# Two heads to a quadrant in two attentions of an eight-layer kernel: row maxima and row sums inside the main products, with a way through DRAM

## The chip, the cores and the metric

The kernel runs on one core of a Trainium2 chip. A core has TensorE (matrix products, into PSUM), VectorE, ScalarE, GpSimd and SyncE, each with its own in-order queue, and 16 DMA engines. DMAs are issued from the queues of SyncE, ScalarE and GpSimd. The metric is the device time of one execution in microseconds; the median of the runs is given. All data is float32.

## The reference, cut to what matters

Four pairs of layers (attention, then feed-forward) are applied in turn to 8 x 512 tokens of 128 features. Each sublayer's input is normalised and its output added to the stream. The change is in the first two attentions and in what the second feed-forward needs before it starts.

```python
# layer 0 attention: 16 heads of 8; in every window of 128 queries the mask
# keeps key j <= i with i counted from the window's start, so only the first
# 128 keys count
scores = einsum('bhqd,bhkd->bhqk', wq, wk) * scale
mask = triu(ones((ws, end), dtype=bool), k=1)
attn = softmax(where(mask, neg, scores), axis=-1)
outs.append(einsum('bhqk,bhkd->bhqd', attn, wv))        # then out @ Wo

# layer 1 attention: 16 heads of 8, 64 features to a head
qf = relu(q @ Wf + bf); kf = relu(k @ Wf + bf)
kv = einsum('blhf,blhd->bhfd', kf, v)
out = einsum('blhf,bhfd->blhd', qf, kv)
normalizer = maximum(einsum('blhf,bhf->blh', qf, kf.sum(axis=1)), 1e-06)
out = (out / normalizer) @ Wo + bo

# layer 1 feed-forward: the best of 16 experts for each token, and a shared one
```

## The kernel before

**One loop for layers 0 and 1.** `l0_l1_ffn` runs the first three sublayers and the second feed-forward's router batch by batch (8 batches of 512 tokens, `P` = 128 partitions, `C` = 4 blocks of 128 tokens). A batch goes through generators, each of which yields between steps: `scores` (normalise, q, k, v, row maxima), then calls of `exps` and `add_up` for r = 0 to 3, then `give` (divide, project with Wo, add), `experts` (layer 0 feed-forward), `features` (layer 1 attention) and `router`. One loop counts `t` from `-LEAD`; a batch has N = 8 values of t, "steps" in the text: `exps(b, r)` is called at t = 8b + 2r, the sums follow one and two steps later, `scores(b)` starts `LEAD` steps ahead, and at each t every live generator is moved by one step. Thus at the same time one batch is in its exponentials, a later one in its scores, earlier ones in experts, features and router. After t = 65 steps of the shared expert (`shared`) fill in. The framework gives every engine a fixed order of instructions close to this program order, and sets all waits.

**Quadrants.** A product with 32 rows or 32 columns uses a quarter of TensorE's array, and four such products, on the four quadrants (`quad(q)`), run side by side. A quadrant holds four heads of 8. To pick head r out of it, `kb[:, r]` is k times a mask `m4` that is zero outside the head.

**Layer 0 attention.** In `scores`, line 486 forms the scores with queries on partitions, ScalarE copies them out (492), GpSimd masks them (493), and VectorE takes the negative maximum of each row (497). The maxima are transposed into `mxT`. In `exps`, line 516 forms the scores again with keys on partitions: for each q the product of `kb` and `qT`, and onto it that of `to_all` and `mxT`, which adds the negative maximum. ScalarE takes exp (523), GpSimd masks (525). In `add_up`, line 539 multiplies `eT` with `vq` (v, zero outside the own head) and, one step later, with `own` (ones instead of v); both accumulate over the four r into `o0` and `o1`. In `give`, VectorE takes the reciprocal of the sums (547) and multiplies (549); two steps later come the projection (554) and the addition.

**Layer 1 attention.** In `features`, line 739 forms kf times v and kf times ones (`one`), for all four heads of a quadrant at once (256 columns), line 744 masks the blocks that belong, a transpose gives `kt`, and line 756 multiplies with qf twice: for the normaliser and for the numerator, each a sum over two halves. Lines 761 to 765 divide; two steps later comes the projection (770).

**The zeros.** Rows of tokens are scattered by expert into `rows_in` in DRAM (`f_in`, 71,680 rows of 512 bytes, line 814, GpSimd's indirect DMA). It must be zero before. Lines 830 to 837 do it with ten DMAs of SyncE, one per step, from the zeroed tile `we`, which `experts` later writes (642). After these, one weight of the list `later` is loaded per step (839).

**The rest.** The experts' products, the layers 2 and 3 with their state-space scan (line 1818) and the output follow after this loop and are not touched. Their line 1182 stores `xh` on ScalarE's queue, and line 1246 loads it again on SyncE's.

## Time and profile before

| | |
|---|---|
| median of 3 runs | 1769.04 us (1764.4 to 1776.76) |
| profiled execution, its own time | 1777.53 us |
| its span, first to last instruction | 1775.8 us |
| mean granted TensorE clock | 0.924 of full |
| TensorE busy | 1523.8 us, 86% |
| VectorE busy | 1208.0 us, 68% |
| ScalarE busy | 785.0 us, 44% |
| GpSimd busy | 675.7 us, 38% |
| start of the layer 0 reciprocal, batches 0 to 7 | 64.9, 94.3, 142.0, 191.1, 273.4, 346.7, 416.6, 478.3 us |

A row of a group has the line, the engine, the operation, the tiles (written <- read), the shapes and the count; after the first bar the busy time in us and the mean of one in ns; after the second the idle time of the engine just before, and what ended it. Busy time of products is modelled and counts overlapping ones once. A row of a stretch has its limits and length, and for each engine the busy time and the number of instructions in it.

### The profile page before, as it was taken

The numbers are of one execution on the slowest core, as the hardware profiler recorded it, in microseconds if no ns is written. First come the engines' busy times: TensorE is split into PE (matmuls) and PEld (weight loads), VectorE is DVE, ScalarE is ACT, GpSimd is POOL, SyncE is SP. The second block draws the span as 40 slices with busy tenths as digits, with TensorE's granted clock in tenths as the row PEclk, the third lists the DMA queues.
The fourth block names the chain that finished last, engine by engine and source line by source line (L and its number), as shares of the span: only waits on it lengthen the run. The fifth ranks groups of instructions, "written<-read, shape, count | busy, mean of one in ns | idle before, by whom it ended". The sixth has DMA issues, their size and how long they took to land.

```text
span 1775.8 us, 22525 instructions
## 1 busy us (share of the span) xinstructions
PE 1523.8 (86%) x8133; PEld 672.7 (38%) x8133; DVE 1208.0 (68%) x2305; ACT 785.0 (44%) x1121; POOL 675.7 (38%) x729
## 2 busy tenths in 40 slices
PE   6978898889999887767999899787888988988877
PEld 2322333334444433554455455332222222333335
DVE  5667647655566543235667665559999999998865
ACT  4545545554454342224223123025555645655644
POOL 5644343342322123021212523425456546641670
PEclk8989888988999998988899899899999999999999
DMA  7990000000000002730554374254444444443301
GB/s 265 383 326 24 1 1 1 13 18 7 7 13 20 17 21 68 222 111 20 127 130 115 100 144 111 80 125 124 140 125 130 129 129 126 126 123 96 82 18 30
DMA packets 98944, 170.92 MB, mean 96 GB/s; under 512 B 11592, under 2 KB 41680, under 8 KB 94736
## 3 DMA queue, kind: packets, MB, share of 16 engines
q1 hardware_dynamic: 94112, 158.20, 31.7%
q0 software_dynamic: 3568, 9.18, 1.7%
q10 hardware_dynamic: 1152, 2.10, 0.4%
q8 instruction: 64, 1.05, 0.2%
q14 instruction: 48, 0.39, 0.1%
HBM read 116.50 MB, written 52.95 MB: 95 GB/s over the span
## 4 chain that ended last, share of the span: by engine, by line
PE 45%; DVE 26%; issue 8%; SPq 6%; DMA 5%; POOL 5%; ACT 4%; DVEq 0%; POOLq 0%; ACTq 0%
DVE h L1818 11%; PE key L1572 5%; PE acc L1550 5%; SPq L833 5%; PE bx L1807 3%; PE sT L516 2%; PE gu L366 2%; PE mm L262 2%; PE o L539 2%; PE Z L1618 1%; DMA gx<-du_d 1%; PE mm L739 1%; PE sc L486 1%; DVE zx L1626 1%; PE mm L1178 1%
## 5 line engine op out<-in xcount | busy, mean ns | idle before, releaser
L1818 DVE TENSOR_TENSOR_SCAN h<-a,bx 128x1024 f32<-128x1024 f32 x192 | 426.5, 2268 | 23.9 <-PE bx L1807 23.7
L1813 ACT ACTIVATE a<-dr,nA 128x1022 f32<-128x1022 f32 x192 | 219.3, 1146 | 217.9 <-DVE h L1818 217.7
L1807 PE MATMUL bx<-gx,wb 64*128 64x512 f32 x768 | 218.8, 662 | 62.4 <-DVE h L1818 59.6
L1263 POOL TENSOR_TENSOR gx<-gx,xk 128x1024 f32<-128x1024 f32 x32 | 75.4, 2358 | 222.2 <-DMA gx<-du_d 212.7
L1572 PE MATMUL key<-xT,L_ffn_keys 128*128 128x512 f32 x256 | 139.6, 628 | 20.2 <-DVE act L1576 20.1
L1807 PEld LDWEIGHTS bx<-gx,wb 64*128 64x128 f32 x768 | 64.6, 194 | 195.6 <-DVE h L1818 149.1
L1550 PE MATMUL acc<-act,L_ffn_values 128*128 128x512 f32 x256 | 134.6, 610 | 0.0
L1576 DVE SCALAR_TENSOR_TENSOR act<-key,gate 128x512 f32<-128x512 f32 x128 | 86.5, 684 | 49.3 <-PE key L1572 37.4
L525 POOL TENSOR_SCALAR_AFFINE_SELECT eT<-eT 128x1024 f32<-128x1024 f32 x64 | 68.6, 1094 | 111.2 <-ACT eT L523 111.2
L1618 PE MATMUL Z<-h,wc 64*32 64x512 f32 x1536 | 109.8, 624 | 1.1 <-DVE h L1818 1.1
L497 DVE TENSOR_REDUCE mx<-sm 128x8 f32<-128x1024 f32 x64 | 76.3, 1212 | 48.1 <-POOL sm L493 48.1
L1361 POOL DMA_INDIRECT back<-f_out,back_at x32 | 30.8, 963 | 167.6 <-DVE bn L248 136.2
L493 POOL TENSOR_SCALAR_AFFINE_SELECT sm<-sm 128x1024 f32<-128x1024 f32 x64 | 69.3, 1096 | 57.9 <-ACT sm L492 57.6
L492 ACT COPY sm<-sc 128x1024 f32<-128x1024 f32 x64 | 63.0, 1013 | 58.7 <-PE sc L486 40.3
L523 ACT ACTIVATE eT<-sT 128x1024 f32<-128x1024 f32 x64 | 62.1, 1020 | 56.6 <-PE sT L516 56.5
L486 PE MATMUL sc<-kb,qT 32*128 32x512 f32 x256 | 61.5, 786 | 23.8 <-ACT eT L523 10.2
L1572 PEld LDWEIGHTS key<-xT,L_ffn_keys 128*128 128x128 f32 x256 | 48.0, 198 | 72.6 <-issue 38.2
L1338 ACT COPY oT<-acc 128x512 f32<-128x512 f32 x8 | 4.7, 586 | 159.3 <-PE acc L1550 159.3
L1550 PEld LDWEIGHTS acc<-act,L_ffn_values 128*128 128x128 f32 x256 | 49.9, 197 | 62.0 <-issue 62.0
L516 PE MATMUL sT<-qT,kb 32*128 32x512 f32 x256 | 57.1, 683 | 14.4 <-ACT sm L492 7.6
L248 DVE BATCH_NORM_STATS2 bn<-x 128x6 f32<-128x128 f32 x224 | 56.2, 271 | 6.5 <-DMA x<-in_L_attn_hidden_states 5.4
L1044 POOL TENSOR_TENSOR rstd<-rstd,minus_half 128x4 f32<-128x4 f32 x27 | 28.0, 1039 | 80.7 <-DVE rstd L1043 80.5
(457 smaller groups left out, 3081.2 us busy)
## 6 DMA issues: line engine op xcount, KB each, us to landing
f_in<-we SPq DMA_DIRECT2D x10, 3584.0 KB
gate<-gates SPq DMA_DIRECT2D x128, 256.0 KB
dr<-dt_d SPq DMA_DIRECT2D x32, 1024.0 KB
gx<-du_d SPq DMA_DIRECT2D x128, 128.0 KB
wt<-in_L_ffn_experts SPq DMA_DIRECT2D x48, 192.0 KB
xk<-xh_d SPq DMA_DIRECT2D x32, 256.0 KB
xg<-f_in SPq DMA_DIRECT2D x48, 64.0 KB
f_out<-ys SPq DMA_DIRECT2D x12, 256.0 KB
```

What stands on the lines that cost most here:

```text
L486: nc.tensor.matmul(halves[q // 2][:, 4 * (q % 2) : 4 * (q % 2) + 4, :], qT[quad(q), cols(c)], kb[quad(q)], start=True, stop=True,)
L497: nc.vector.tensor_reduce(mx[:, c, 2 * i : 2 * i + 2, 0:4], sm.rearrange("p (q r) k -> p q r k", q=2), AX.X, ALU.max, negate=True,)
L516: nc.tensor.matmul(halves[q // 2][:, q % 2, :], lhs[quad(q), r, :], rhs[quad(q)], start=(k == 0), stop=(k == 1),)
L833: nc.sync.dma_start(rows_in[per * (t - 1) : per * t, :].rearrange("(p n j) d -> p n (j d)", p=P, j=4), we.rearrange("p c k e -> p (c k e)" ...
L1263: nc.gpsimd.tensor_tensor(gx, gx, xk.unsqueeze(1).to_broadcast([P, 2, S]), ALU.mult)
L1550: nc.tensor.matmul(acc, f2_v[:, j, :], act, start=(j == 0), stop=(j == J - 1))
L1572: nc.tensor.matmul(key, f2_k[:, 2 * j : 2 * j + 2, :], xT, start=True, stop=True)
L1576: nc.vector.scalar_tensor_tensor(act, key, 0.0, gate[:, j % 2, :], ALU.max, ALU.mult)
L1618: nc.tensor.matmul(zs[q][32 * j : 32 * j + 32, i, :], wcf[half, g, :], hs[j // 2][half, j % 2, :], start=(g == 0), stop=(g == G - 1),)
L1807: nc.tensor.matmul(bx[:, k, :], wbf[half, g, :], gx[half, j, :], start=True, stop=True,)
L1813: nc.scalar.activation(a[:, :, 1:], dr[:, 2 * j : 2 * j + 2, 1:], AF.Exp, scale=nA[:, q, g : g + 1],)
L1818: nc.vector.tensor_tensor_scan(h.rearrange("p r t -> p (r t)"), a.rearrange("p r t -> p (r t)"), bx.rearrange("p r t -> p (r t)"), 0.0, AL ...
```

## The change

**Two heads to a quadrant, maxima in the same product.** q is stored to DRAM so that 16 of the 32 rows of a quadrant hold two heads, and two more rows hold these heads' negative maxima; two loads (`qm`) bring both forms back, one for the first and one for the second pair of heads. `k2` has k of one head in its 8 rows and a one in the row of that head's maximum; it is made from a second projection with a padded weight `wk2`. `exps` then needs one product for each q instead of two. `qs`, the two DRAM buffers, are zeroed once at the start.

**Sums in the same product.** `vq` has 32 columns for two heads: 8 of v, 8 of ones, for each. The sums of r = 0, 1 and r = 2, 3 go to two accumulators; each is copied out by ScalarE, stored to DRAM from ScalarE's queue (`halves_out`), and `rejoined` loads numerators and denominators back as two tiles. The reciprocal comes one step after these loads. Layer 1's attention is built in the same way: `v1` has v and ones side by side, a product has 128 columns instead of 256, line 756's products are half as many, and the result goes through DRAM; its division comes two steps after the loads, its projection one step later than before.

**Zeros in groups.** 35 DMAs of 1 MB, seven at each of t = 2, 10, 18, 26, 34, from a tile `nought` of 1 KB per partition, a column of which GpSimd rewrites from the newest `eT` before each group. The weights of `later` follow after the last group. `LEAD` is 14 instead of 13.

The diff, cut to its core:

```diff
+                wk2 = keep.tile([P, 2, 4, 32], F32, tag="wk2", name="wk2")
...
+                qs = [dram.tile([4, 2, 32, S], F32, tag=f"qs{i}", name=f"qs{i}") for i in range(2)]
+                for t in qs:
+                    nc.scalar.dma_start(
+                        t.rearrange("q r x (h t) -> (q r x h) t", h=2).rearrange("(n p) t -> p n t", p=P),
+                        nought.unsqueeze(1).to_broadcast([P, 4, 2 * D]),
+                    )
...
+                def halves_out(od, r, o, ov):
+                    nc.scalar.copy(ov, o)
+                    nc.scalar.dma_start(od[:, r], ov)
+
+                def rejoined(od):
+                    vd = work.tile([P, 2, S], F32, tag="vd", name="vd", bufs=3)
+                    src = od.rearrange("q r (e s d) t -> (q r e) s d t", e=2, s=2)
+                    for s in range(2):
+                        nc.sync.dma_start(vd[:, s], src[:, s])
+                    return vd
...
+                    nc.scalar.dma_start(rows[:, 0:16, :], qT)
...
+                    for i in range(2):
+                        nc.tensor.matmul(
+                            mm[:, cols(2 + i)], wk2[:, i].rearrange("p q x -> p (q x)"), xT[:, 0:P],
+                            start=True, stop=True,
+                        )
...
+                    k2 = work.tile([P, 2, 2, P], F32, tag="k2", name="k2", bufs=2)
+                    for e in range(2):
+                        nc.vector.tensor_scalar(
+                            k2[:, :, e, :], mm[:, 2 * P :].rearrange("p (r k) -> p r k", r=2),
+                            ones_at, mk[:, e : e + 1], ALU.add, ALU.mult,
+                        )
...
+                    nc.scalar.dma_start(rows[:, 16:18, :], mxT)
+                    qm = []
+                    for i in range(2):
+                        qm.append(work.tile([P, S], F32, tag=f"qm{i}", name="qm"))
+                        nc.sync.dma_start(qm[i], qs[b % 2][:, i])
...
-                    for k, (lhs, rhs) in enumerate(((kb, qT), (to_all, mxT))):
-                        for q in range(4):
-                            nc.tensor.matmul(
-                                halves[q // 2][:, q % 2, :], lhs[quad(q), r, :], rhs[quad(q)],
-                                start=(k == 0), stop=(k == 1),
-                            )
+                    for q in range(4):
+                        nc.tensor.matmul(
+                            halves[q // 2][:, q % 2, :], k2[quad(q), r // 2, r % 2, :],
+                            qm[r // 2][quad(q)], start=True, stop=True,
+                        )
...
                         nc.tensor.matmul(
-                            o[quad(q)], vq[:, q, r, :] if i == 0 else own[:, r, :],
-                            eT[q // 2][:, q % 2, :], start=(r == 0), stop=(r == 3),
-                        )
+                            o[quad(q)], vq[:, q, r, :], eT[q // 2][:, q % 2, :],
+                            start=(r % 2 == 0), stop=(r % 2 == 1),
+                        )
+                    if r % 2:
+                        od, ov = sums_of[b]
+                        halves_out(od, i, sums_of.pop((b, i)), ov[:, i])
...
                 def give(b):
                     ready.pop(b)
-                    nc.vector.reciprocal(rd, sums_of.pop((b, 1)))
...
+                    vd = rejoined(sums_of.pop(b)[0])
+                    yield True
+                    aT, rd = vd[:, 0], vd[:, 1]
+                    nc.vector.reciprocal(rd, rd)
+                    nc.vector.tensor_tensor(aT, rd, aT, ALU.mult)
...
-                    for k in (1, 0):
-                        for i in range(2):
-                            for q in range(4):
-                                nc.tensor.matmul(
-                                    o[quad(q), k, :], kt[:, 2 * k + i, quad(q)], qf[:, q, i, :],
-                                    start=(i == 0), stop=(i == 1),
-                                )
+                    for i in range(2):
+                        for q in range(4):
+                            nc.tensor.matmul(
+                                o[quad(q), i, :], kt[:, i, quad(q)], qf[:, q, i, :],
+                                start=True, stop=True,
+                            )
+                    od = dram.tile([4, 2, 32, S], F32, tag="od1", name="od1", bufs=2)
+                    ov = work.tile([P, 2, S], F32, tag="vd", name="ov", bufs=3)
+                    nc.scalar.copy(ov, o)
+                    for i in range(2):
+                        nc.scalar.dma_start(od[:, i], ov[:, i])
+                    vd = rejoined(od)
+                    yield True
+                    yield True
...
-                LEAD = 13
+                LEAD = 14
...
+                    if t % 8 == 2 and t > 0 and fills:
+                        nc.gpsimd.tensor_scalar(
+                            nought[:, 0:1], last[0][:, 0, 0:1], 0.0, None, ALU.mult
+                        )
+                        for rows in (fills.pop() for _ in range(7)):
+                            nc.sync.dma_start(
+                                rows.rearrange("(p n j) d -> p n (j d)", p=P, j=2),
+                                nought.unsqueeze(1).to_broadcast([P, PER // (2 * P), 2 * D]),
+                            )
+                    elif t > 0 and not fills and later:
+                        nc.sync.dma_start(*later.pop(0))
...
-                        if (b, r) in waiting:
-                            add_up(b, r, 1, waiting[b, r])
```

## The prediction

> **What bounds the kernel now.** I read the slices of the page first, then the kernel cut at the ends of the first attention's batches, then the chain of one such batch, then the groups that the change touches, and last the queue that carries the fills. The cuts are the starts of the eight reciprocals of line 547 (64.9, 94.3, 142.0, 191.1, 273.4, 346.7, 416.6, 478.3 us); the loop's last work ends near 665 us. In the stretches the columns are TensorE (PE), its weight loads, VectorE, ScalarE, GpSimd, then the granted clock, the DMA share and GB/s.
>
> ```profile
> 65.00:94.00 29.00, 27.84 (x185) 10.77 (x186) 22.24 (x39) 18.22 (x22) 19.65 (x20) 1.00 1.03 383
> 94.00:142.00 48.00, 36.81 (x198) 12.96 (x196) 29.54 (x66) 21.62 (x26) 21.79 (x23) 0.82 0.89 282
> 142.00:191.00 49.00, 40.76 (x219) 14.27 (x218) 32.89 (x81) 25.67 (x32) 24.21 (x26) 0.90 0.00 0
> 191.00:273.00 82.00, 73.27 (x414) 28.17 (x408) 46.25 (x112) 40.83 (x48) 28.74 (x31) 0.85 0.00 1
> 273.00:347.00 74.00, 65.50 (x406) 27.38 (x406) 46.57 (x110) 38.02 (x47) 27.22 (x30) 0.91 0.02 8
> 417.00:478.00 61.00, 57.15 (x366) 25.28 (x362) 34.59 (x97) 28.26 (x35) 21.11 (x24) 0.89 0.03 10
> 478.00:665.00 187.00, 168.00 (x956) 80.75 (x950) 110.93 (x295) 83.47 (x106) 42.70 (x51) 0.93 0.05 17
> ```
>
> TensorE is busy 77 to 96% of every stretch, VectorE at most 77% (65:94), ScalarE and GpSimd less. So TensorE comes first, but with 4 to 11 us of idle time per batch that other engines' chains make. The chain of waits from 273 to 347 us says the same: products are its largest part (10.9% on line 516, 6.3% on 539, 4.9% on 739), yet from 330 to 347 us it runs through short VectorE steps of the first experts' gating and the two 3.3 us reciprocals, which the change keeps. Work taken from TensorE is therefore worth something in every batch, but not all of it.
>
> ```profile
> L516 PE MATMUL sT<-mxT,to_all 32*128 32x512 f32 x256 | 53.6, 636 | 0.0
> L539 PE MATMUL o<-eT,own 128*32 128x512 f32 x256 | 45.3, 650 | 0.0
> L756 PE MATMUL o<-qf,kt 128*32 128x512 f32 x256 | 29.4, 595 | 3.1 <-ACT sm L492 2.3 <-ACT kt L265 0.8
> L739 PE MATMUL mm<-kf,v 128*32 128x256 f32 x256 | 17.9, 403 | 0.4 <-ACT lg L786 0.4
> L739 PE MATMUL mm<-kf,one 128*32 128x256 f32 x256 | 16.0, 379 | 0.0
> ```
>
> These rows (groups by shape, 0 to 700 us; a product is two records) are the work that goes or halves: busy us, mean ns, idle before.
>
> **The change part by part.** *Score products.* The pass that adds the maxima (to_all by mxT) goes: four products in each of 32 calls. The row says 53.6 us, 1.68 a call, but the four run side by side and the records' ends overlap: at full clock their two waves start 0.43 us apart, so 0.86 us, 0.97 at the stage's clock of 0.89. I take 1.35, between: 32 x 1.35 = 43 us. *Sums.* The products with own go: 45.3 us by the row; a call of lines 539's two sets takes 8.74 us for eight sets in 65:94 (1.09 each) and 10.2 to 10.5 for eight later (1.3). I take 1.25: 40 us. *Linear attention.* The 64 records of line 739 per batch stay, on 128 columns instead of 256: 33.9 us halved is 17, less something for short products: 15. Line 756 goes from 32 to 16 records a batch: 29.4 halved, 15. *Added.* Two products of 128 columns with wk2 per batch: line 466's like product costs 0.46 us a batch, so 8 x 0.93 = 7, less overlap, 5. Two transposes of km fewer a batch (5.1 us halved): -2.5. TensorE's sum is 43 + 40 + 15 + 15 - 5 + 2.5 = **110 us**; bounds 85 (pitch alone) and 132 (all the busy time).
>
> *Beside other work.* VectorE loses vq (0.68) and half of km (0.35) and gains two k2 (256 elements from PSUM, some 0.35 each) and two small copies: zero. ScalarE gains two copies of 512 columns (2 x 0.59) and six DMA issues (0.33 each, the row below) per batch, and half a microsecond for the double-width copy of o: 4 us on 38 of 74, hidden by TensorE. If that cover went, it would be 30 us in all. The set-up adds some ten GpSimd fills of 0.1 to 0.5 us: 3 us beside the wait for the weights.
>
> *The way through DRAM.* Each batch stores qT, mxT and o and loads qm and vd back, and its linear part does so once more. The nearest rows are the scan's store on ScalarE's queue and the load that waits for it:
>
> ```profile
> L1182 ACTq DMA_DIRECT2D xh_d<-xh x8: 326/326/345, 991.2 to 1527.5; - x8
> L1246 SPq DMA_DIRECT2D xk<-xh_d x32: 516/525/631, 993.7 to 1647.8; - x32
> ```
>
> The first store is issued at 991.2 us and SyncE's load at 993.65: 2.4 us. A load lands some 2.8 us after issue (the first x: 0.81 to 3.58). With two issues the round trip is 2.4 + 1.0 + 2.5 = 6 us. For the scores it has two steps of an eighth of a batch (8 to 18 us): hidden. For the sums it has one step before the reciprocal and two before line 554: copy 0.6 + 6 + reciprocal 3.35 + product 0.6 = 10.5 against two steps of 8 to 9 in the early batches (late by 1 to 2 us, three times: 4 us), nothing later. In the linear part it has two steps before the reciprocal: hidden while a step is 7 to 9 us, about 1 us late in each of the four batches of the tail, where it is 3.8 (187 us over 49 steps): 4 us. Its projection also comes one step later, felt once at the end: 4 us. What waits behind on VectorE when vd is late is mx and kf, and TensorE behind those.
>
> *The fills.* Now ten DMAs of 3.5 MB run from 19 to 115 us, and the first write of we waits for them:
>
> ```profile
> L833 SPq DMA_DIRECT2D f_in<-we x10: 1773/9242/10037, 19.4 to 92.3; - x10
> DVE we L642 <- DMA L_ffn_shared_up_w<-in_L_ffn_shared_up_w: 11.8, 1, 11.8
> ```
>
> That wait ends at 120 us (its label is the queue's next transfer). It goes; TensorE is idle 11 us in that stretch against 8 in the next, so I credit 3. After, 35 fills of 1 MB in five groups of seven follow exps of batches 0 to 4, in packets of 1 KB. The trace has 27 ns for 512 bytes, 65 for 1536 and 86 for 2048; in between 46 ns, so a group is 7 x 64 x 46 ns = 20.6 us. Bounds: 19.2 (the rate of 383 GB/s) and 38.5 (a packet costs 86 ns whatever its size). SyncE's queue is in order: qm of the next batch, asked for four steps after the group, stands behind it. With a period T, the load comes at T/4 + 2 (the eT that gates it) + 20.6 + 4, and is needed at T: T is at least 35 us. That binds only in 65:94, now 29 us: +6. (At 38.5 us a group T is at least 59, which would put the first three periods at +30, +11 and +10: the whole change near zero. It goes into the range.) Later loads now start at step 35; the first user (the router of batch 0, near step 44) is behind that. A store on ScalarE's queue during a fill: with busy SyncE traffic xh_d's packets were spread over 8 to 9 us instead of 0.8, but there against packets of 8 KB. The Trainium skill (DMA: Bandwidth & Descriptors, Queues, rings and completion order) says an engine alternates between queues packet by packet; then small fill packets cost a store 1 us. By the row each exposed store would cost 8, by the rule 1. I take the rule, since those 8 KB packets are unlike these; only mxT's store would matter, and its load is behind the fills anyway.
>
> *The clock.* The skill (TensorE: Matmul & The Clock Gate, Part 1) speaks against the change: after an idle window of some 3.4 us TensorE runs at half clock. If each of the 16 round trips left it idle so long, a half-clock window of 3.4 us would cost 1.7 us each: 27 us. The rows show 1.00 where idle is 1 us, 0.82 at 11, but also 0.85 at 9 and 0.90 at 8. Since other products fill these steps, I take nothing beyond the share below.
>
> **The sum.** Per full batch 110/8 = 14 us leave TensorE. What of it is on the chain of 273 to 347: 516's 8.1 us times 1.35/3.46, half of 539's 4.7, half of 739's 3.6, under 1 of 756's: 7 to 8. So between 7.5 and 14; I take 10. Stretches: 0 to 65: -2. 65 to 94: +6. To 142: -7 - 3. To 191: -8. The next three -10 each, to 478: -9. The tail has four linear parts left, 4 x 3.8 = 15 on a TensorE that is 90% busy: -13. Delays from DRAM +4 and +4, last step +4. Together **-54 us**. The profiled execution took 1777.53 us; the median is 1769.04. 54 us off the median: **1715 us**. Nothing after 665 us changes.
>
> **Rivals.** *TensorE really is the bound*: the 132 us of busy time and the wait on we go almost whole, 100 to 125 us: 1655. For it: 94 to 96% busy in 65:94 and 417:478. Against: VectorE's 47 us of 74 with in-order chains. Chance 0.13. *The gain stays off the chain*: only the gating chain counts, 5 us a batch, 40 us, and DRAM (12), fills (6) and clock (27 by the rule) take it back: 1774. For: 330 to 347 us runs without TensorE. Chance 0.13. *The way through DRAM stands in line.* The place is VectorE's queue at the two reciprocals, where vd is awaited; mx and kf stand behind, and TensorE behind them. The price is a whole round trip of 6 us in each of 16, 96 us where I counted 8: 88 us worse, 1803. It decides from where the 54 us are used up: 8 + 54 over 16, that is 3.9 us late each time. For: queues in order, one step of slack before give's reciprocal, and SyncE's queue shared with fills and weights. Against: a step of 6 to 9 us from batch 2 on is as long as the trip. Chance 0.14. *My forecast* (gains of 18 to 100 us): 0.60.
>
> **How the numbers follow.** Faster than 1% (18 us) is about what a measurement can tell from none. Faster: the forecast and the first rival, 0.73; within 1%: 0.13; slower: 0.14. The range takes the bounds of TensorE's sum below and reaches into no gain above: 1650 to 1780.
>
> **What would show it.** After: line 516 and 539 with half their records; the starts of give's reciprocal some 10 us closer from the fourth batch on, and 6 us further apart between the first two; no wait of we; the tail near 185 us; the scan unchanged. Wrong if VectorE waits for vd above 2 us a batch, if TensorE's first score products wait for qm above 3 us in the full batches, or if the stretches shrink by under 5 us.

## The result, and the profile after

The kernel after takes **1894.13 us** (median of 4, 1890.17 to 1898.64) against 1770.38 us for the kernel before on the same chip: a ratio of 1.070 [1.065, 1.074], 124 us slower. The forecast was 1715. The profiled execution took 1898.64 us, with a span of 1896.9 and a mean granted clock of 0.862.

The stretches, cut as before at the starts of the layer 0 reciprocal (now line 614: 100, 161, 212, 268, 350, 427, 505, 568 us). The columns are those of the prediction's first fence.

```profile
0.00:100.00 100.00, 52.47 (x200) 19.45 (x200) 36.30 (x85) 35.78 (x41) 40.36 (x77) 0.77 0.64 188
100.00:161.00 61.00, 46.34 (x152) 15.99 (x148) 30.05 (x67) 25.18 (x31) 25.85 (x29) 0.61 0.49 157
161.00:212.00 51.00, 36.10 (x150) 13.22 (x151) 30.18 (x68) 26.60 (x33) 21.97 (x24) 0.70 0.56 181
212.00:268.00 56.00, 45.38 (x184) 18.55 (x182) 32.83 (x79) 25.27 (x34) 22.28 (x25) 0.74 0.51 167
268.00:350.00 82.00, 64.25 (x302) 27.43 (x302) 44.90 (x98) 37.85 (x45) 25.51 (x27) 0.73 0.36 119
350.00:427.00 77.00, 62.71 (x338) 27.54 (x336) 46.07 (x112) 39.91 (x49) 27.30 (x30) 0.81 0.15 46
427.00:505.00 78.00, 61.95 (x300) 29.09 (x299) 43.34 (x103) 36.43 (x44) 28.70 (x30) 0.68 0.16 45
505.00:568.00 63.00, 50.24 (x288) 23.58 (x285) 34.70 (x99) 30.11 (x36) 18.21 (x22) 0.79 0.14 43
568.00:800.00 232.00, 175.87 (x871) 88.88 (x872) 107.86 (x311) 83.53 (x109) 56.08 (x86) 0.79 0.12 35
```

The count of TensorE's instructions (the first number in brackets) fell as it should: 302 where 414 stood in the fifth stretch. But TensorE is now busy in 71 to 81% of the batches from the second on, where it was 77 to 96%, and the clock column reads 0.61 to 0.81 where it read 0.82 to 1.00. No stretch became shorter. Nearly all the loss lies in the loop of layers 0 and 1: the 32nd scatter of the router, the loop's last work, moved from 688 to 805 us; from there to the end it is 1092 us after and 1088 before.

The groups by shape: first the two rows of the kernel before that the prediction did not show (0 to 700 us), then the kernel after, 0 to 805 us (line 574 was 516, 601 was 539, 805 was 739, 824 was 756):

```profile
L516 PE MATMUL sT<-qT,kb 32*128 32x512 f32 x256 | 57.1, 683 | 14.4 <-ACT sm L492 7.6 <-DVE kf L713 5.6 <-ACT qf L730 0.8
L539 PE MATMUL o<-eT,vq 128*32 128x512 f32 x256 | 44.6, 659 | 0.0
```

```profile
L574 PE MATMUL sT<-qm,k 32*128 32x512 f32 x256 | 79.4, 864 | 58.0 <-DMA qm<-qs 46.8 <-ACT sm L544 6.1 <-ACT qf L794 4.8
L601 PE MATMUL o<-eT,vq 128*32 128x512 f32 x256 | 49.6, 776 | 0.0
L805 PE MATMUL mm<-kf,v 128*32 128x128 f32 x512 | 20.8, 316 | 4.1 <-DVE x L386 3.9 <-ACT v L649 0.2
L824 PE MATMUL o<-qf,kt 128*32 128x512 f32 x128 | 17.6, 656 | 0.2 <-ACT kt L819 0.2
```

The products with the maxima and with `own` are gone. What is left got longer: a record of the score product takes 864 ns, 683 before; one of the sums 776, where it was 650 and 659. And the score product waits 46.8 us for `qm`. The waits of VectorE and of SyncE's queue, 0 to 805 us (total, times, longest):

```profile
DVE vd L837 <- DMA vd<-od: 64.8, 8, 11.9
DVE vd L614 <- DMA vd<-od: 41.1, 4, 16.3
...
SPq L563 <- DMA qs<-mxT: 163.7, 8, 45.8
SPq L494 <- DMA od<-ov: 159.3, 17, 24.0
```

VectorE waits for the rejoined sums in all eight linear parts (64.8 us) and in four of the eight divisions (41.1). With `qm` that is 152.7 us of waits behind the way through DRAM, where the prediction had counted 8. A wait of an engine is not yet time of the kernel. The chain of waits of one batch (268 to 350 us) shows that here it is on the path: the store of `od` and the load of `vd` are 18.7% of it, 15.3 of 82 us.

```profile
by line: issue 16.8%; DMA od<-ov 14.2%; PE sc L538 11.1%; PE sT L574 7.6%; DVE kf L777 5.6%; DMA vd<-od 4.5%; PE mm L735 4.4%; DVE vd L614 4.0%; DVE mx L549 2.9%; ACT qf L794 2.7%; PE o L601 2.5%; PE mm L505 2.4%; PE mm L262 2.3%; ACT kf L7
```

What it is worth in all, experiments had to price.

### The profile page after: what moved, and what is told of

Same layout as the page of the kernel before. It is cut to its first block, busy times and chain, and to the rows that moved or that the text cites. A ratio compares the mean times of both kernels' runs of the same rounds, so it can differ in the third digit from the quotient of the medians.

```text
span 1896.9 us, 21537 instructions
## 1 busy us (share of the span) xinstructions
PE 1522.6 (80%) x7509; PEld 685.5 (36%) x7509; DVE 1211.7 (64%) x2332; ACT 795.8 (42%) x1134; POOL 679.1 (36%) x741
## 4 chain that ended last, share of the span: by engine, by line
PE 45%; DVE 19%; DMA 14%; issue 10%; ACT 5%; POOL 5%; SPq 1%; ACTq 0%; DVEq 0%; POOLq 0%
DVE h L1897 9%; DMA od<-ov 5%; PE key L1651 5%; PE acc L1629 4%; PE bx L1886 3%; PE sc L538 3%; DMA gx<-du_d 3%; PE sT L574 2%; DMA vd<-od 2%; PE mm L262 2%; PE gu L371 2%; PE o L601 2%; PE Z L1697 1%; DMA gate<-gates 1%; PE qq L789 1%
## 5 line engine op out<-in xcount | busy, mean ns | idle before, releaser
L574 PE MATMUL sT<-qm,k 32*128 32x512 f32 x256 | 79.4, 864 | 58.0 <-DMA qm<-qs 46.8
L538 PE MATMUL sc<-kb,qT 32*128 32x512 f32 x256 | 86.7, 930 | 35.4 <-DVE kf L777 21.9
L782 ACT ACTIVATE kf<-kf 128x2048 f32<-128x2048 f32 x16 | 30.6, 1910 | 104.4 <-DVE kf L777 104.3
L262 PE MATMUL mm<-ident,xn 128*128 128x128 f32 x160 | 33.4, 345 | 35.6 <-DVE xn L352 24.0
```

Of the source, the lines that this page charges most:

```text
L262: nc.tensor.transpose(ps[:, c, :], src[:, c, :], ident)
L538: nc.tensor.matmul(halves[q // 2][:, 4 * (q % 2) : 4 * (q % 2) + 4, :], qT[quad(q), cols(c)], kb[quad(q)], start=True, stop=True,)
L574: nc.tensor.matmul(halves[q // 2][:, q % 2, :], k2[quad(q), r // 2, r % 2, :], qm[r // 2][quad(q)], start=True, stop=True,)
```

## The experiments

Four theories were tried. **A**: the two ways through DRAM are on the path, because few DMA engines carry them (A1) or because loads stand behind something else in SyncE's queue (A2). **B**: the start is late, as the first fill and the later weights stand ahead in SyncE's queue. **C**: TensorE's granted clock fell, as the smaller products leave it idle more often. **D**: the grouped fills disturb. All ratios are to the kernel before, taken on the same chip. Four runs (the sums' products put back, the two on the parts that are left and the order of queues, and the maxima alone) were on a second chip, so they are set against the others by ratio.

### Without one way, without the other, without both

The division runs on the copy `ov` in place (sums and values are not brought together), or the score product reads a constant instead of q with the maxima, or both.

```diff
 # e1: no way for the sums              # (e3: both edits)
-                    nc.scalar.dma_start(od[:, r], ov)
-                    vd = rejoined(sums_of.pop(b)[0])
+                    vd = sums_of.pop(b)[1]
-                    for i in range(2):
-                        nc.scalar.dma_start(od[:, i], ov[:, i])
-                    vd = rejoined(od)
+                    vd = ov
 # e2: no way for q and the maxima
-                    nc.scalar.dma_start(rows[:, 0:16, :], qT)
-                    nc.scalar.dma_start(rows[:, 16:18, :], mxT)
-                        nc.sync.dma_start(qm[i], qs[b % 2][:, i])
+                    qm = fixed
```

> The kernel after, with the way of the numerators and denominators through DRAM left out in both attentions: the store and the loads go, and the division works on the copy as it stands (rows in the wrong places). Theory A (the round trips of the sums stand in VectorE's queue: 106 us of waits for vd in the kernel after, most of it with TensorE idle behind): 80 to 110 us less, 1785 to 1815. Theory B (the loss is made at the start, by weights and fills that stand ahead of the first loads of the maxima in SyncE's queue): at most 30 us less, above 1860. Theory C (TensorE's clock fell, whatever waits): under 15 us.

> The kernel after, with the way of q and the maxima through DRAM left out: the two stores and the two loads go, and the exponentials use a constant tile in place of qm. Theory A (sums): 15 to 45 us less, since TensorE waits 47 us for qm but part of that time would be lost to vd anyway. Theory B (start): 50 us or more less, for nothing of the first attention stands behind weights or fills any more except vd. Theory C (clock): under 15 us.

> The kernel after, with both ways through DRAM left out (constant tile for qm, division on the copy as it stands). What is left is the smaller work of TensorE and the fills in groups. Theories A and B: the gain that was forecast for TensorE shows, 1690 to 1725 us. Theory C (the smaller products themselves leave TensorE idle and at half clock): above 1770.

| run | us | ratio [95%] | against after |
|---|---|---|---|
| without the sums' way | 1780.85 | 1.0045 [1.0019, 1.0072] | -113 |
| without the maxima's way | 1849.09 | 1.0431 [1.0373, 1.0490] | -45 |
| without both | 1751.41 | 0.9877 [0.9820, 0.9934] | -143 |

So the way through DRAM costs 143 us, give or take 10: the sums' way 98 to 113 of them, the maxima's 29 to 45, by which of the two is left out first. And with both gone for nothing, the change gains only about 21 us, where the forecast implies 62 (its 54 and the 8 that it counted for the trips); the first run gave a little more than theory A's 80 to 110 us, the second the edge of its 15 to 45, the third lies in neither of its expectations. Theory C had under 15 us for each of the first two and falls as the first cause; the clock comes back below. Two things were wrong, not one.

### The later weights held back

```diff
-                        nc.sync.dma_start(*later.pop(0))
+                        dst, put = later.pop(0)
+                        nc.gpsimd.tensor_scalar(one, last[0][:, 0, 0:1], 0.0, None, ALU.mult)
+                        nc.sync.dma_start(dst, put)
```

(`one` is the first column of `dst`: the load has to wait for this write.)

> The kernel after, with each of the later weights' loads held back by a small write of GpSimd into its tile from the newest exponentials, so that they come after the last fill, as the program's text has it, and not from 21 us on, ahead of the first fill, where the trace has them. Theory B (start): the first score products, which wait until 62 us for qm behind the 5 us load of keys and the others, come 15 to 25 us earlier, and the time falls by 15 to 30 us. Theory A: the same 15 to 20 us at most, and the waits for vd stay at about 100 us. Theory C: nothing.

1891.63 us, 1.0684 [1.0622, 1.0746]: within the noise of the kernel after. The first exponentials came only 4 us earlier (at 50.1 us for 54.3; 39.8 in the kernel before), and the waits for `vd` stayed (107.7 us for 105.9). So the later weights are not the cause, and as the whole delay of the start is 14.5 us, a late start makes up directly no more than that of the 124: theory B falls as the main cause.

### 128 rows in one run: how many DMA engines carry a store

In the kernel after, `od` and `qs` lie in DRAM as [4 quadrants][2][32 rows], and one store or load touches `od[:, r]`: an outermost dimension of 4. Here the order is [2][4][32], so that each store of `od` and each load of `qm` is one run of 128 rows (the stores of q and of the maxima keep an outermost dimension of 8, the loads of `vd` one of 16). The columns of Wq and Wk and the rows of both Wo are laid out to match; everything else is as in the kernel after.

```diff
-qs = [dram.tile([4, 2, 32, S], F32, tag=f"qs{i}", ...) for i in range(2)]
+qs = [dram.tile([2, 4, 32, S], F32, tag=f"qs{i}", ...) for i in range(2)]
-                    nc.scalar.dma_start(od[:, r], ov)
+                    nc.scalar.dma_start(od[r].rearrange("q x t -> (q x) t"), ov)
-                        nc.sync.dma_start(qm[i], qs[b % 2][:, i])
+                        nc.sync.dma_start(qm[i], qs[b % 2][i].rearrange("q x t -> (q x) t"))
```

> The kernel after with another order of the same rows in DRAM and of the weights, so that the stores of o and the loads of qm are one run of 128 rows instead of 4 separated blocks of 32 rows. In the kernel after, a store's 128 packets of 84 ns take 5.2 us of time where 16 engines would need 0.7, and the load behind it is issued 9 to 11 us after the store. Theory A1 (the trips are long because a transfer with 4 outer blocks uses only a few of the 16 DMA engines, the same ones for stores and loads): from store to load some 3 us, waits for vd and qm halved or better, 60 to 110 us less than 1894. Theory A2 (they are long because other waits stand ahead in SyncE's queue): under 20 us less.

1795.79 us, 1.0148 [1.0085, 1.0211]: **98 of the 143 us come back**. Nothing was changed but the order of rows in DRAM, and with it the shape of the transfers. The waits, 0 to 805 us:

```profile
PE sT L574 <- DMA qm<-qs: 14.9, 5, 6.9
...
DVE vd L614 <- DMA vd<-od: 12.0, 3, 6.6
DVE vd L837 <- DMA vd<-od: 10.3, 6, 2.4
```

46.8, 41.1 and 64.8 us have become 14.9, 12.0 and 10.3. The DMA view shows why. First the kernel after, 120 to 160 us (a value a microsecond): mean busy share of the 16 engines in tenths, and what they moved.

```profile
DMA  9991000121210000044200001010222222220089
GB/s 348 346 347 34 0 0 0 18 14 49 104 76 0 0 0 0 0 47 102 113 0 0 0 0 33 0 12 27 70 53 88 102 98 106 98 104 27 23 213 312
```

In the first three microseconds a fill runs at some 347 GB/s with the share at 9 tenths or more. From 148 to 156 us the two loads of `qm`, issued from 145.5 on, and the second store of `od`, issued at 145.8, run together at some 100 GB/s, with the share at 2 tenths, from which I estimate that 4 of the 16 engines worked. The same stretch of the kernel with 128 rows, 110 to 150 us:

```profile
DMA  0000700000000044100000108791197005999999
GB/s 3 0 0 0 262 0 0 0 0 0 0 0 0 0 53 143 66 0 0 0 0 0 33 0 74 244 406 64 25 317 182 0 16 201 328 321 351 327 353 346
```

`qm` and `od` (issued from 133.42 and at 133.7) pass in 3 us, at up to 406 GB/s, and `vd` after them at 317. The time from the store's issue to the load's, in the tile views of `od`, the kernel after first, then this one:

```profile
L494 SPq DMA_DIRECT2D vd<-od x2: 547/570/592, 156.6 to 157.2; - x2
L487 ACTq DMA_DIRECT2D od<-ov x1: 542/542/542, 145.8 to 145.8; - x1
```

```profile
L487 ACTq DMA_DIRECT2D od<-ov x2: 326/326/326, 133.7 to 163.6; - x2
L494 SPq DMA_DIRECT2D vd<-od x2: 561/576/592, 137.3 to 137.9; - x2
```

145.8 to 156.6 is 10.8 us; 133.7 to 137.3 is 3.6. The single packets bear the estimate out. In both kernels they have 2 KB and take 84 ns (median). From 150 to 155 us of the kernel after four are under way for three quarters of the time and never more than six, although both queues have transfers running; with 128 rows, from 134 to 137 us, it is mostly sixteen or more while they run. The Trainium skill states the rule (DMA: Bandwidth & Descriptors, "Why a DMA increments its semaphore by 16 and not by 1", and "Use all 16 engines" in its table of rules): the number of engines is the largest up to 16 that divides the slowest dimension of both sides, 4 here and 16 with 128 rows, and on this kind of queue it is always the lowest-numbered ones. Four packets under way agree with the 4, and that it stays four with both queues running agrees with their using the same engines; which of the 16 they are no run here shows. Some 44 us of the two ways remain (1795.79 against 1751.41), and what makes them up was not taken apart.

### The fills

The run without either way gets the ten fills from `we` of the kernel before (e6); the kernel before gets the 35 fills in five groups (e8).

```diff
 # e8; e6 is the reverse
-                    if 0 < t <= 10:
-                        nc.sync.dma_start(rows_in[per * (t - 1) : per * t, :]..., we...)
+                    if t % 8 == 2 and t > 0 and fills:
+                        nc.gpsimd.tensor_scalar(nought[:, 0:1], last[0][:, 0, 0:1], 0.0, None, ALU.mult)
+                        for rows in (fills.pop() for _ in range(7)):
+                            nc.sync.dma_start(rows..., nought...)
```

> Both ways through DRAM left out, as in the run without them (1751), and the zeros filled as in the kernel before (ten DMAs from we, no wait for the exponentials). Theory D (the fills in groups hold the first batches, whose distance is 44 us against 29 before): 15 to 25 us less, 1725 to 1737. Theory C (TensorE's half-clock makes those first batches slow): within 8 us of 1751, or slower by the wait of we.

> The kernel before with the zeros filled in five groups of seven from a tile of their own, as in the kernel after, and nothing else. Theory D: the first batches' distance grows and it is 5 to 20 us slower. My own sum: the wait of we goes (3 us) and nothing waits for the fills: 1765 to 1770.

1758.74 us (0.9909 [0.9880, 0.9937]) where the grouped fills gave 1751.41 (0.9877 [0.9820, 0.9934]): the intervals overlap. And 1770.27 us, 0.9978 [0.9960, 0.9995], on the kernel before: by the interval 1 to 7 us faster. Theory D falls, and with it the prediction's +6; its -3 for the wait of `we` fits.

### What the work taken out is worth when it is put back

```diff
 # e7: the score product twice (the scores are doubled)
+                    for k in range(2):
                         for q in range(4):
-                            ... qm[r // 2][quad(q)], start=True, stop=True,
+                            ... qm[r // 2][quad(q)], start=(k == 0), stop=(k == 1),
 # e9: the product with vq twice
+                    for q in range(4):
+                        nc.tensor.matmul(o[quad(q)], vq[:, q, r, :], eT[q // 2][:, q % 2, :], ...)
```

> Both ways through DRAM left out (1751), and the score products of the exponentials issued twice, so that TensorE has as many of them as in the kernel before, with no other engine's work changed. If the removed pass was worth its 30 to 43 us: 1780 to 1795. Theory C (the clock takes back what the smaller work gives): under 15 us more, with a higher granted clock in the first 500 us.

> The kernel without either way through DRAM (1751 us), with every product of values and sums issued twice into the same accumulation, so the output of the first two attentions is doubled (256 more TensorE products over the eight batches, as many as the change took out). Theory 'the removed sums were on TensorE's path': the prediction priced them at 40 us, so about 1790 us and a ratio near 1.01 to the kernel before. Theory 'the removed sums ran in TensorE's waits for ScalarE's exponentials': they go back into those waits and cost 0 to 12 us, so 1751 to 1763 us.

The score pass costs 35 us (1786.08, 1.0077 [1.0055, 1.0099]), inside the first expectation; against theory C, which had under 15. The sums' products cost some 20 by ratio (1769.88, 0.9991 [0.9971, 1.0011]), between the two expectations and half of the 40 in the prediction. Both carry the 10 us of noise of the run that they are set against. Together that is some 55 us put back into a kernel that had gained only 21. So either some 30 us went into parts that the change adds, or work put in costs more than the same work taken out gains.

### Parts that are left of the way, and the order of queues

```diff
 # e10: the kernel without either way, and ...
-                    nc.scalar.dma_start(t..., nought...)      # zero fill of qs
-                LEAD = 14
+                LEAD = 13
 # (and the division one or two steps earlier again)
 # e12: the kernel with 128 rows, and ...
-                    nc.sync.dma_start(xT_d[b], xT)
+                    nc.scalar.dma_start(xT_d[b], xT)
```

> The kernel without either way through DRAM, and also without what is left of that way: the zero fill of the places in DRAM at the start, the one step more of lead and the later division (the sums and maxima are still not brought to their places, as in the run without either way). Theory 'the late start and the later division ate the gain': first products about 5 us earlier, each batch 1 us shorter, 1735 to 1743 us. Theory 'TensorE's waits for ScalarE in the first batches ate it': the start alone comes back, 1744 to 1751 us.

> The kernel with 128 contiguous rows to a store and load (1796 us), and the router's store of xT moved from SyncE's queue to ScalarE's. Theory 'SyncE stands at that store, and the loads of maxima and sums behind it': the waits for qm (15 us) and for the sums' load shrink by half or more, 1775 to 1787 us. Rival 'only the number of engines mattered, the rest is the two trips themselves': 1792 to 1800 us; if ScalarE's own work then waits at the store, over 1800 us.

1746.90 us (0.9830 [0.9770, 0.9889]), below the run without either way (0.9877) but with overlapping intervals: the late start and the later division are a small matter. 1800.62 us (1.0159 [1.0088, 1.0229] against 1.0148 with 128 rows): the router's store was not what loads stood behind, and A2 falls as far as this store goes. That SyncE "waits" 217 us at it with 128 rows cost nothing that can be measured; in the kernel before it waits 425 us at the same store.

### The maxima alone, with the way through DRAM

The kernel before with the score passes merged, in 128 rows; sums, division and fills as before; `wk2`, the zeroing of `qs` and LEAD 14 as in the kernel after.

```diff
-for k, (lhs, rhs) in enumerate(((kb, qT), (to_all, mxT))):
-    ... start=(k == 0), stop=(k == 1)
+    ... k2[quad(q), r // 2, r % 2, :], qm[r // 2][quad(q)], start=True, stop=True
+ # qT and mxT stored to qs[b % 2], qm loaded from it, as in the kernel after
```

> The kernel before with only the maxima of the two heads in one product (the score pass merged, 128 contiguous rows to a store and a load of DRAM); sums, division and fills as before. Theory 'the way of the sums through DRAM and the few engines cost it all': score pass worth 35 us less about 15 us of waits for the maxima and 5 us at the start: 1750 to 1760 us, ratio 0.99 to 0.995. Rival 'one trip through DRAM ahead of the scores already costs what the pass saves': 1765 to 1785 us.

1791.98 us, 1.0100 [1.0069, 1.0131], worse than both expectations. Even with loads in one run of 128 rows, a trip ahead of the scores, with the projection and the earlier lead that go with it, costs more than the pass it saves. The wait for `qm` is 9.1 us (three times, 5.9 at most), the later start about 10 (first reciprocal at 74.5 us, 64.8 before); what makes up the rest was not taken apart.

### Only taking out

Here the kernel before loses products and gains nothing: no pass for the maxima, and the sums from one call of four (f1). Then also 12 of the 32 products of line 739 and 4 of the 16 of line 756 in each batch (f2). The output lacks these parts.

```diff
 # f1, in the kernel before
-for k, (lhs, rhs) in enumerate(((kb, qT), (to_all, mxT))):
+halves <- kb[quad(q), r, :] x qT[quad(q)] alone
-o[quad(q)] <- vq[:, q, r, :] if i == 0 else own[:, r, :]
+o[quad(q)] <- vq[:, q, r, :] if i == 0, or `one` if i == 1 and r == 0
 # f2: kv for k == 1 from c == 0 alone; o for k == 1 from i == 0 alone
```

> The kernel before without the pass that adds the maxima to the scores and with the sums taken from the first of the four heads alone (224 of 256 such products gone); nothing is added, order and lead stay. Theory 'the added parts outside the way through DRAM ate about 30 us': the removal is worth what the two products cost when put back, 35 and 16 us, so about 1720 us, ratio 0.971. Theory 'the products removed were covered by ScalarE's and VectorE's chains': as in the run without either way, 1745 to 1755 us.

> The same, and in the linear attention 12 of the 32 products of line 739 and 4 of the 16 of line 756 in each batch left out, so the features' sums are incomplete. The prediction priced all of this work at 30 us of TensorE; what is left out here is 12.7 us of the one row and 7.4 of the other, 20 us. Theory 'TensorE bounds the linear part': 14 to 20 us below the run without these edits. Theory 'VectorE's gating chain and the router bound that part': 0 to 6 us below it.

1752.11 us (0.9890 [0.9852, 0.9928]) and 1751.17 (0.9891 [0.9851, 0.9930]). The second expectation holds in both: **the removal by itself brings 17 us (13 to 26 by the interval), and the linear part's share nothing that can be measured**, about what the whole change brings without its way through DRAM (21). So the parts that the change adds outside this way ate nothing beyond the noise; the gain was not there to be eaten. If anything f1 flatters the removal, as its sums are complete after the first call and the division may come earlier. The stretches up to and from the 32nd scatter, the kernel before and then f1:

```profile
0.00:688.00 688.00, 595.21 (x3376) 252.10 (x3377) 403.73 (x987) 329.61 (x404) 264.00 (x337) 0.89 0.21 73
688.00:1776.00 1088.00, 928.57 (x4758) 420.64 (x4756) 804.29 (x1318) 455.35 (x718) 411.68 (x392) 0.94 0.42 111
```

```profile
0.00:665.00 665.00, 556.37 (x2930) 235.53 (x2931) 401.28 (x988) 330.56 (x404) 264.75 (x338) 0.88 0.22 76
665.00:1765.00 1100.00, 941.10 (x4757) 428.20 (x4755) 805.41 (x1318) 455.62 (x717) 411.56 (x392) 0.93 0.42 110
```

446 records fewer (56 calls: 32 of the maxima, 24 of the 32 of the sums) take only 595.2 - 556.4 = 39 us off TensorE's busy time, where the prediction's prices give 43 + 30 = 73 (30 is 24 of 32 calls of its 40): 0.7 us a call of four. TensorE's idle time grows from 93 to 109 us, so 23 of the 39 reach the scatter. What takes over is seen in the chain of waits of one batch, the kernel before (273 to 347 us) and f1 (260 to 331):

```profile
by line: PE sT L516 10.9%; DVE rd L547 8.8%; PE sc L486 8.8%; PE o L539 6.3%; PE mm L739 4.9%; DVE mx L497 4.7%; DVE kf L713 4.6%; DVE rd L764 4.3%; PE mm L660 3.9%; issue 3.1%; ACT qf L730 3.0%; PE qq L725 2.9%; PE mm L554 2.7%; PE mm L653
```

```profile
by line: PE sc L486 11.0%; PE sT L515 7.7%; PE o L761 7.4%; PE mm L744 5.1%; PE mm L675 4.9%; DVE kf L718 4.8%; DVE rd L552 4.6%; DVE rd L769 4.5%; PE o L539 4.0%; PE mm L665 4.0%; ACT qf L735 3.2%; PE qq L730 3.0%; issue 3.0%; PE mm L559 2
```

The score product of the exponentials (which lost a half) and the sums (which lost three eighths) fall from 17.2 to 11.7% of the chain. The other lines on it, scores, features, experts and two reciprocals, are all still there, and from one reciprocal to the next it is 71.8 us instead of 73.3.

### The maxima merged with no way through DRAM

The same merging in the kernel before, without a trip: two copies of qT with the rows of the other head pair set to zero (GpSimd), onto which VectorE adds the transposed maxima, masked by partition, straight from PSUM. The heads' order in `kb` is turned so that the maxima come to rows 16 and 17 of a quadrant for the first pair, 0 and 1 for the second; `k2` is `kb` with ones in these rows.

```diff
+for i in range(2):
+    nc.gpsimd.tensor_scalar(qm[i], qT, mp[:, i : i + 1], None, ALU.mult)
+nc.gpsimd.tensor_tensor(k2, kb, at_r.unsqueeze(2).to_broadcast([P, 4, P]), ALU.add)
-flipped(mx.rearrange("p c q r -> p c (q r)"), mm_four(), mxT)
+    nc.vector.scalar_tensor_tensor(qm[i], mm, mp[:, 1 - i : 2 - i], qm[i], ALU.mult, ALU.add)
-for k, (lhs, rhs) in enumerate(((kb, qT), (to_all, mxT))):
+    ... k2[quad(q), (r + 2) % 4, :], qm[r // 2][quad(q)], start=True, stop=True
```

> The kernel before with the maxima merged into the score product, but brought to their places by VectorE and GpSimd, with no DRAM: per head pair a copy of q with the other pair's rows set to the maxima (masks by partition), two VectorE operations of 512 columns and three of GpSimd more a batch, no other edit. Theory 'the pass is worth 35 us and only the way through DRAM spoiled it': VectorE's additions (2 x 0.7 us a batch, mostly hidden) take back 4 to 8, so 1740 to 1748 us, ratio 0.983 to 0.988, faster than both kernels. Rival 'the gain stays behind VectorE's chains': 1760 to 1772 us.

1762.43 us, **0.9949 [0.9928, 0.9970]**: 7 us below the kernel before, a small gain but clear of the noise, and 132 below the kernel after. That lies in the range of the rival, "the gain stays behind VectorE's chains" (1760 to 1772), and not in that of the first theory (1740 to 1748): the way through DRAM was not all that kept the pass from paying. The removal of the pass and of most sums together had brought 17.

```profile
L472 POOL TENSOR_SCALAR qm<-qT,few 128x512 f32<-128x512 f32 x16 | 25.1, 1575 | 3.6 <-ACT qT L469 3.6
L517 DVE SCALAR_TENSOR_TENSOR qm<-mm,few,qm 128x512 f32<-128x512 f32 x16 | 11.0, 731 | 1.1 <-PE mm L515 1.1
```

The price is 2 x 0.73 us of VectorE a batch and GpSimd's 2 x 1.6, with the addition for `k2`, beside other work. The trip of the maxima alone gave 1.0100 for the same merged product.

## Why the prediction was wrong

**The way through DRAM: the step that failed first.** The prediction took 2.4 us from store to load from the row of `xh_d`, 6 us for the whole trip, and judged all but 8 us hidden. The row was of another shape: that store goes in one run of 128 rows, while `od[:, r]` has 4 blocks. In the stretch shown, the step took 10.8 us with its real shape and 3.6 with 128 rows. Late `vd` then cost VectorE 106 us of waits in 12 places, and late `qm`, which the prediction had called hidden behind two steps, TensorE 47. The third rival named the right place, VectorE's two reciprocals with TensorE behind, and for the 16 trips of the sums a price near the truth, 96 us, where 98 to 113 were measured; it had 0.14. The size is in part luck: it took 6 us at each of 16 places, and the runs show longer trips that were waited for at 12. It fell short of 1894 because it still took the 54 us of gain from the rest and left `qm` out. The miss of 179 us (1894 for 1715) divides into the trips, 143 measured for 8, and the rest, 1751 measured without the trips where the prediction has 1707: 135 and 44.

The prediction weighed rules for a store beside a fill and for the clock, and none for the shape of the stores. The rule on the number of engines spoke against the change, and the layout was in the diff.

**TensorE's 110 us: the second step that failed.** Up to the 32nd scatter the kernel without the two ways has 49 us less of TensorE's busy time than the kernel before (595.2), at a lower clock; its row and that of the kernel after:

```profile
0.00:667.00 667.00, 545.99 (x2757) 240.38 (x2758) 410.68 (x1015) 343.80 (x422) 268.73 (x351) 0.84 0.24 77
0.00:805.00 805.00, 600.32 (x2773) 266.04 (x2774) 408.13 (x1018) 341.86 (x421) 267.60 (x350) 0.75 0.30 93
```

Score pass and sums were put at 83 us, with 85 for all as the lowest bound. Taking them out, but for the one call in four kept for the sums (73 us by the same price), freed 39 us of busy time. Busy time here is a union in which neighbouring products overlap. A group's 53.6 or 45.3 us is thus not what leaves with it: what stays takes longer (up to 480 us, line 756's record is 595 ns in the kernel before and 707 in f1, with the products the same). Whether that is the neighbours' spreading into the gap or the somewhat lower clock (0.88 for 0.89 up to the scatter) was not separated. The linear part's 30 us was priced at 14 to 20 for the share that was tried, and brought 1. Of the three rivals and the forecast, "the gain stays off the chain" came nearest with 40 us on the chain, still twice what was found.

**How much of it counts.** 10 of 14 us a batch were to be realised. With f1's removal the first exponentials start at 39.8 us as before and the last at 438.7 instead of 468.4: 30 us over eight batches, below 4 a batch. The last scatter keeps 23 of them, and the median at the end 17. (The part after the scatter is 1088 us before and 1100 in f1, but f1's profiled execution, 1766.6 us, was the slowest of its four, so this stays open.)

**The clock.** The prediction took nothing beyond a share, against the rule's 27 us. It had weighed the rule by the idle time of whole stretches, while the rule is about one idle window; single waits behind the trips last up to 15.7 us (`qm`) and 16.3 (`vd`). The products that run up to the 32nd scatter are nearly the same in the two rows above (2773 and 2757 records): 600.3 us of TensorE at a granted clock of 0.75 against 546.0 at 0.84. So 54 us of product time is the slower clock and what goes with it, and TensorE was as busy as before (595.2) with 600 records fewer. The records of the clock know two values only, full and half, and change at multiples of 3.41 us, as the rule has it; up to the 32nd scatter they are at half for 147 us before, 218 without the ways and 399 after. The estimate of one window of 3.4 us at each of 16 trips, 54 us at half clock, was thus far too small, even for the 181 us that the ways alone make. How much of this is on the path cannot be told from the waits it comes with. The direction was the rule's.

**What was right.** The fill group of 20.6 us (22 measured in four of the five and 31 in the first; packets of 1 KB take 48 to 50 ns) and that fills alone do not decide. The wait of `we` is gone. After the loop no more than 4 us changed. What a store beside a fill costs, 1 us by the rule or 8 by the row, no run isolates. The signs named for a failure, VectorE waiting for `vd` above 2 us a batch (13.2) and TensorE for `qm` above 3 (5.9), are the ones that showed.

## What to carry to other kernels

Before a trip through DRAM is priced by another store's row, compare the shapes: a tile's outermost dimension of 4 sends it over 4 of 16 engines, and a layout that makes it one run of 128 rows took 98 of 143 us off. Before TensorE's work is priced by its group's busy time, take some of it out and look: here, where calls are small and many chains share the engine, about half of the group's busy time was freed (39 of 73 us), and about half of that reached the end (17). And where something has only to change its partition within 32 rows, try a transposing product with a mask and an addition before a trip: for the maxima it gave 0.9949 where the trip, with what it brings along, gave 1.0100.

## What the runs showed of the hardware that was not expected

A transfer on few engines does not only take longer itself: from 148 to 156 us two loads and a store that were issued within 0.7 us on two queues shared one rate of some 100 GB/s and four packets under way, while a fill over all engines moves 347. TensorE's granted clock over the loop fell from 0.89 to 0.84 with the smaller work alone and to 0.75 with the trips, and the record of a score product went from 683 to 740 and 864 ns. And the same pass of products was worth different times by direction, though in two different kernels: 35 us when put in, 17 for it and most of the sums' products together when taken out.
